# The zero margin of a DRAM table moved from GpSimd's queue to SyncE's, and the first image's normalized rows split over VectorE and ScalarE

## The chip, the core and the metric

The kernel runs on one core of a Trainium2 chip. The core has TensorE (PE), VectorE (DVE), ScalarE (ACT), GpSimd (POOL) and SyncE (SP), and 16 DMA engines that move data between DRAM and the core's SBUF. SP computes nothing: it issues DMAs. POOL issues DMAs too, through a queue of its own. The metric is the device time of the whole program in microseconds (us).

## The reference

The network takes four images of 256 channels by 64 by 64 positions and applies four residual blocks to each. Each block normalizes its input by groups of eight channels and adds a layer's output to the image. Cut to what matters here, the first block is:

```python
def _gn(v, G=32, eps=1e-5):                    # (g - mean) / sqrt(var + eps) by groups of 8 channels
    ...
def _L0_conv_ref(x, offset_w, offset_b, mod_w, mod_b, weight):   # K2 = 9 taps
    offset = _conv(x, offset_w, offset_b)      # 3x3 convolution, 18 channels: a shift per tap
    mask = 2.0 * sigmoid(_conv(x, mod_w, mod_b))
    return _deform_conv2d(x, offset, mask, weight)   # bilinear samples at shifted places, zero outside

x = x + _L0_conv_ref(_gn(x), ...)   # layer 0, deformable convolution
x = x + _L1_conv_ref(_gn(x), ...)   # layer 1, attention
x = x + _L2_conv_ref(_gn(x), ...)   # layer 2, deformable, in groups
x = x + _L3_conv_ref(_gn(x), ...)   # layer 3, a state-space scan
```

A sample of layer 0 blends the four neighbours of a fractional place. Places beyond the image count as zeros.

## The kernel before

Channels lie on the 128 partitions, in two halves `ct` (0 and 1). The image `x` stays in SBUF as 128 x 2 x 4096 floats. The images are computed one after another. For images 1 to 3 layer 0's preparation is done inside the layers of the image before (`known` is set). For image 0 nothing is known, and the preparation stands at the very start of the program. The change concerns that start.

The start of image 0 goes as follows.

1. `fetch` (L109) issues 16 DMAs of 256 KB on SP's queue, each 128 rows of 2 KB: eight chunks of `x`, two channel halves each. Behind them on the same queue come `ident`, `gmat`, `goff` and `base` (L138, L90), then the offset convolution's weights `l0`, the deformable convolution's weights `l0w` (128 x 4608 floats) and layer 1's weights `l1`.
2. `borders` (L114) zeroes the margin of `tab`, a table in DRAM of 4,547 rows of 1,024 floats. The rows hold, for each place of the zero-padded 66 x 66 image, the channels of its four neighbours. The first `FAR` = 67 rows and the 67 rows from row 4,480 are the margin. The source is a zeroed tile `zero` of 67 partitions by 256 floats, read four times for each row. POOL issues the two DMAs.
3. `note` (L218) takes statistics of each chunk of `x` on DVE as it lands. `stats` joins them with two small matmuls (L254, L269), a square root on ACT (L273) and a reciprocal on DVE (L274).
4. `scaled` (L289) writes the normalized rows into the padded image `xnp` with 16 DVE instructions, each of 8 rows and one channel half.
5. `table` (L406 to L414), called for t0 = 0, 5, ..., 30, transposes 5 x 128 places on PE, copies them to a tile `vt` (of which there are two) on ACT and DVE, and writes `vt` four times to `tab`, at row offsets that make the four neighbours. SP issues these 7 x 4 = 28 DMAs of 640 KB, in rows of 1 KB. The offset convolution (`offsets`, L371, two rounds of 72 matmuls here) stands between the transposes of t0 = 10 and 15, and of t0 = 20 and 25.
6. `biases` (L128) loads small constants of layer 2 through POOL (`pick`, `halves`, `bom3v`, `bv3v`). Their tiles take the place of the `vt` tiles, so the DMA of `halves` waits until all table writes have landed.
7. `along` (L489) gathers rows of `tab` by indirect DMAs that POOL issues, and the rest of layer 0 follows from these.

The order of the start on each engine is fixed by a scheduler when the program is built; at run time the engines wait for each other by semaphores. DMAs that SP issues use eight completion semaphores in turn: a DMA waits until the one issued eight before it on the queue has landed. A DMA that writes rows of `tab` that an earlier one wrote waits for it as well. The four writes of t0 = 0 start at rows 67, 66, 1 and 0, so the second of them overlaps the first margin and waits until that has landed.

Of the kernel before, what the change touches and what calls it, by code (L numbers as in the profile page):

```python
# [9 lines left out]
F32 = mybir.dt.float32  # L10
I32 = mybir.dt.int32
BF16 = mybir.dt.bfloat16
AF = mybir.ActivationFunctionType
ALU = mybir.AluOpType
AX = mybir.AxisListType

P = 128
H = W = 64
N = H * W
PW = 66  # L20
FAR = PW + 1
# [3 lines left out]
FT = -(-PW * PW // P)  # L25
# [38 lines left out]
class Net:  # L64
# [7 lines left out]
    def __init__(self, ctx: ExitStack, tc: tile.TileContext, ins: dict[str, bass.AP]):  # L72
        self.tc, self.nc, self.ins = tc, tc.nc, ins
        nc = tc.nc
        self.cpool = ctx.enter_context(tc.tile_pool(name="const", bufs=1))
        self.xpool = ctx.enter_context(tc.tile_pool(name="x", bufs=1))
        self.small = ctx.enter_context(tc.tile_pool(name="small", bufs=2))
        self.dram = ctx.enter_context(tc.tile_pool(name="dram", bufs=2, space=bass.MemoryType.DRAM))

        self.x = self.xpool.tile([P, 2, N], F32, tag="x", name="x")  # L80
        self.fetched = False
        self.fetch()
        self.eps = self.cpool.tile([P, 1], F32, tag="eps", name="eps")
        nc.gpsimd.memset(self.eps, 1e-5)
        self.ones = self.cpool.tile([P, P], F32, tag="ones", name="ones")
        nc.gpsimd.memset(self.ones, 1.0)
        for name in ("ident", "gmat", "goff"):
            setattr(self, name, self.load(self.cpool, name))
        self.base = self.cpool.tile([P, 8, 18], F32, tag="base", name="base")
        nc.sync.dma_start(out=self.base, in_=ins["base"][:, 0:8, :])  # L90
        self.first = self.spot(self.cpool, 0)
        self.awake = False
        self.omax = self.cpool.tile([P, 1], F32, tag="omax", name="omax")
        nc.gpsimd.memset(self.omax, 0.0)

        self.halves = self.cpool.tile([3, 3, P], BF16, tag="halvesb", name="halvesb")
        self.noted = None


        self.tab = self.dram.tile([FAR + FT * P, 1024], F32, tag="tab", name="tab", bufs=1)  # L100
        self.known = None
        self.pick = None
# [11 lines left out]
    def borders(self):  # L114

        nc = self.nc
        with self.tc.tile_pool(name="zero", bufs=1) as pool:
            zero = pool.tile([FAR, 1, 256], F32, tag="zero", name="zero")
            nc.gpsimd.memset(zero, 0.0)
            for r in (0, FT * P):  # L120
                nc.gpsimd.dma_start(
                    out=self.tab[r : r + FAR, :].rearrange("p (s c) -> p s c", s=4),
                    in_=zero.to_broadcast([FAR, 4, 256]),
                )

    def biases(self):

# [207 lines left out]
    def layer0(self, x, weights):  # L335


        nc, tc = self.nc, self.tc
        tab, known, self.known = self.tab, self.known, None
        with (  # L340
# [11 lines left out]
            if not known:  # L352
                for r in borders:
                    nc.gpsimd.memset(r, 0.0)
                self.borders()
                self.scaled(x, lambda ct: [(self.inner(ct, r, 8), r, 8) for r in range(0, H, 8)])
            cw, cb = self.loads(px, "l0", nc.gpsimd if known else None)
            wf = self.load(pa, "l0w")
            weights()
            spots = [self.first] + [self.spot(pa, i) for i in range(1, 4)]  # L360
# [72 lines left out]
            with (  # L433
# [16 lines left out]
                if known:  # L450
                    put = lambda q, do: after.setdefault(q, []).append(do)
                    gm, rs = known
# [1609 lines left out]
```

## Time and profile before

| | us |
|---|---|
| median of three runs | 8874.15 (8865.99 to 8879.99) |
| the profiled execution, its own time | 8914.06 |
| span of the profiled execution on the core | 8912.3 |
| busy: PE, DVE, POOL, ACT | 8069.4, 7767.5, 6963.3, 4998.0 |
| statistics of the last chunk of `x` begin (L218) | 24.54 and 25.56 |
| the 16 DVE instructions of `scaled` (L289) | 29.21 to 36.59 |
| first and last issue of a table write (L414) | 37.32 and 84.56 |
| `halves` is issued by POOL (L138) | 94.21 |
| first gather is issued (L489) | 96.01 |

Times in the profile run from the start of the span. A row of the timeline gives the start, the duration, the engine, the line of the code, the operation with what it writes and reads, and the count of merged instructions. SPq marks DMAs that SP issues; the duration is that of issuing, not of the transfer. The profiled execution is longer than the median of the runs by 0.45%.

### The profile page before, as it was taken

How to read it: one execution, taken by the hardware profiler on the slowest of the kernel's cores; microseconds unless marked ns; L12 is line 12 of the kernel's file. 1: busy time of each engine (PE TensorE's matmuls, PEld its weight loads, DVE VectorE, ACT ScalarE, POOL GpSimd, SP SyncE). 2: the span in 40 equal slices, each digit the busy share in tenths (PEclk: the TensorE clock that was granted, in tenths of full speed). 3: DMA queues.
4: the chain of work that ended last, by engine and by line, in shares of the span. 5: the costliest groups of instructions: out<-in, count | busy, mean ns of one | idle time of the engine just before them, and what ended most of it. 6: DMA issues, size and time to landing. Idle time of an engine off the chain costs nothing.

```text
span 8912.3 us, 97084 instructions
## 1 busy us (share of the span) xinstructions
PE 8069.4 (91%) x31127; PEld 4255.1 (48%) x31127; DVE 7767.5 (87%) x9908; ACT 4998.0 (56%) x7610; POOL 6963.3 (78%) x4415
## 2 busy tenths in 40 slices
PE   5789998998878999999887899999988799999997
PEld 4653474443555347444356435634435643564443
DVE  5778798999877879899987887999997778889998
ACT  4753435666675343666667434376666743446664
POOL 4747697999674779799967577989996747788998
PEclk8999999999999999999999999999999999999999
DMA  8850011445884011244588301124458820112332
GB/s 298 309 196 12 31 61 57 112 111 142 297 311 160 10 37 59 65 114 113 156 297 319 122 13 43 60 80 112 110 170 307 315 80 1 47 61 76 107 107 80
DMA packets 457945, 1149.69 MB, mean 129 GB/s; under 512 B 51426, under 2 KB 119019, under 8 KB 446161
## 3 DMA queue, kind: packets, MB, share of 16 engines
q0 software_dynamic: 178800, 681.04, 23.1%
q1 hardware_dynamic: 278624, 462.37, 16.8%
q8 instruction: 248, 4.06, 0.2%
q14 instruction: 273, 2.23, 0.1%
HBM read 905.84 MB, written 88.10 MB: 112 GB/s over the span
## 4 chain that ended last, share of the span: by engine, by line
DVE 32%; PE 32%; POOL 13%; issue 11%; ACT 5%; DMA 5%; SPq 2%; another core or an unknown queue 1%; DVEq 0%; POOLq 0%; ACTq 0%
DVE h L1886 16%; PE cx L715 10%; DVE h L1802 6%; POOL h L1909 5%; DMA g<-tab,idx 3%; PE sc L685 3%; PE pm L595 3%; PE pz L537 3%; POOL g L489 2%; PE pacc L1039 2%; SPq L892 2%; DVE prod L1014 2%; DVE r L500 2%; ACT r L499 1%; PE y L1763 1%
## 5 line engine op out<-in xcount | busy, mean ns | idle before, releaser
L1909 POOL TENSOR_TENSOR h<-h,cn 128x2048 f32<-128x2048 f32 x508 | 2300.2, 4528 | 41.3
L1886 DVE TENSOR_TENSOR_SCAN h<-da,carry,h 128x512 f32<-128x512 f32 x1636 | 1983.0, 1265 | 77.7 <-ACT da L1884 28.5
L1884 ACT ACTIVATE da<-delta,l3a 128x512 f32<-128x512 f32 x2048 | 1397.4, 691 | 1053.2 <-DVE h L1886 1049.4
L1763 PE MATMUL y<-h,ident 128*128 128x512 f32 x4096 | 1913.5, 600 | 5.1 <-POOL h L1909 4.0
L489 POOL DMA_INDIRECT g<-tab,idx x1152 | 1364.1, 1184 | 564.8 <-DVE r L500 288.4
L709 POOL TENSOR_TENSOR acc<-acc,e 128x1024 f32<-128x1024 f32 x472 | 1109.9, 2352 | 352.7 <-ACT e L700 333.7
L537 PE MATMUL pz<-cols,l0w 128*128 128x256 f32 x4608 | 1207.4, 406 | 154.0 <-DVE cols L526 77.7
L1763 PEld LDWEIGHTS y<-h,ident 128*128 128x128 f32 x4096 | 780.7, 192 | 1013.1 <-issue 946.5
L500 DVE SCALAR_TENSOR_TENSOR r<-g,wx,r 128x512 f32<-128x512 f32 x1152 | 859.4, 746 | 324.6 <-ACT r L499 198.5
L537 PEld LDWEIGHTS pz<-cols,l0w 128*128 128x128 f32 x4608 | 875.9, 201 | 360.2 <-issue 123.8
L700 ACT ACTIVATE e<-e 128x1024 f32<-128x1024 f32 x512 | 542.2, 1059 | 898.6 <-DVE e L699 785.7
L715 PE MATMUL cx<-e,v 128*128 128x512 f32 x2048 | 1002.1, 615 | 2.3 <-ACT e L700 2.3
L1802 DVE TENSOR_TENSOR h<-du,bn 128x1536 f32<-128x1536 f32 (+1 forms) x512 | 937.4, 1831 | 4.0 <-PE bn L1787 3.9
L499 ACT ACTIVATE r<-g,wx 128x512 f32<-128x512 f32 x1152 | 828.1, 719 | 195.9 <-DMA g<-tab,idx 153.5
L1014 DVE TENSOR_TENSOR prod<-ring,A 128x768 f32<-128x768 f32 (+1 forms) x640 | 715.6, 1160 | 49.3 <-DMA ring<-ring 29.5
L699 DVE TENSOR_TENSOR e<-sc,mr 128x512 f32<-128x512 f32 x1024 | 638.5, 681 | 126.6 <-PE sc L685 126.6
L1039 PE MATMUL pacc<-ident,prod 128*128 128x128 f32 x5120 | 663.9, 280 | 49.9 <-POOL prod L1028 19.4
L608 DVE TENSOR_REDUCE m<-pm 128x1 f32<-128x512 f32 x896 | 555.5, 682 | 110.8 <-PE pm L595 110.8
L519 PE MATMUL pt<-ident,acc 128*128 128x128 f32 x2304 | 420.5, 290 | 254.2 <-DVE acc L510 191.8
L715 PEld LDWEIGHTS cx<-e,v 128*128 128x128 f32 x2048 | 350.2, 189 | 603.5 <-issue 435.3
L1039 PEld LDWEIGHTS pacc<-ident,prod 128*128 128x128 f32 x5120 | 562.5, 142 | 139.8 <-POOL prod L1028 50.6
L509 ACT ACTIVATE acc<-r,wy 128x256 f32<-128x256 f32 x1152 | 574.5, 499 | 40.5 <-DVE r L500 38.7
(307 smaller groups left out, 11989.1 us busy)
## 6 DMA issues: line engine op xcount, KB each, us to landing
cn<-cd SPq DMA_DIRECT2D x512, 256.0 KB
bs<-cd SPq DMA_DIRECT2D x412, 256.0 KB
delta<-du POOLq DMA_DIRECT2D x48, 1024.0 KB
tab<-vtnext SPq DMA_DIRECT2D x192, 256.0 KB
ring<-ring SPq DMA_DIRECT2D x288, 126.0 KB
ring<-ring SPq DMA_DIRECT2D x288, 120.0 KB
delta<-w POOLq DMA_DIRECT2D x24, 1024.0 KB
g<-tab,idx POOLq DMA_INDIRECT x1152
```

The lines of the kernel that those rows point to most:

```text
L489: nc.gpsimd.indirect_dma_start(out=g[:], out_offset=None, in_=tab[:, :], in_offset=bass.IndirectOffsetOnAxis(ap=spots[t // 8][0][:, t % 8, ...
L499: nc.scalar.mul(r, g[:, :, 0, :], wx[:, 0, t, k : k + 1])
L500: nc.vector.scalar_tensor_tensor(r, g[:, :, 1, :], wx[:, 1, t, k : k + 1], r, ALU.mult, ALU.add)
L537: nc.tensor.matmul(sums[m][:, ot, :256], wf[:, i, bass.ts(ot, P)], cols[m][:, i, :], start=(i == 0), stop=(i == 17),)
L709: nc.gpsimd.tensor_add(b["acc"], b["acc"], e)
L715: nc.tensor.matmul(blocks[qb]["cx"], v[:, 4 * (i + kt // 4 * 4) + kt % 4, :], e[:, bass.ts(i % 2, 512)], start=(kt == 0 and i == 0), stop= ...
L1039: nc.tensor.matmul(d["pd"][:, ct, t, :], prod[:, x, t, bass.ts(ct, P)], self.ident, is_transpose=True, start=(wy == 0 and x == left[0] and ...
L1763: nc.tensor.matmul(c["ys", dc], self.ident, h[:, dc, :], start=False, stop=(n == DS - 1))
L1802: nc.vector.tensor_mul(h[:, :d, :], c["du"][:, :d, :], c.pop(("bn", n)).to_broadcast([P, d, C]))
L1884: nc.scalar.activation(da, c["delta"][:, dc, :], AF.Exp, scale=al[:, dc, n : n + 1])
L1886: nc.vector.tensor_tensor_scan(h[:, dc, :], da, hb, carry[:, dc, n : n + 1], ALU.mult, ALU.add)
L1909: nc.gpsimd.tensor_mul(h, h, cn.to_broadcast([P, 4, C]))
```

## The change

`zero` becomes a tile of the constants' pool with 64 floats on each of 67 partitions, zeroed once by POOL at the start. `borders` is called later, after the load of `l0`, and SP issues its two DMAs, each reading the 64 zeros 16 times for each row. On SP's queue they stand behind `x`, `ident`, `gmat`, `goff`, `base` and `l0`, and ahead of `l0w`, `l1` and the 28 table writes. POOL's two margin DMAs are gone, and its DMA of `pick` moves up.

The normalized rows of image 0 are shared: channel half 0 stays on DVE with 8 instructions, half 1 goes to ACT as 8 activations `scale * x + shift`, with a small DVE instruction that computes the shift `-mean * rs`. ACT and DVE copies of `vt`, and the small steps of the offsets, change places among each other on their engines by a few positions. PE's order is the same, and so is the order of every engine after the start. The code for the general layer 2, which the program only runs under a condition, changes in the same way.

```diff
@@ __init__
         self.awake = False
+        self.zero = self.cpool.tile([FAR, 1, 64], F32, tag="zero", name="zero")
+        nc.gpsimd.memset(self.zero, 0.0)
         self.omax = self.cpool.tile([P, 1], F32, tag="omax", name="omax")
@@ def borders(self):
-        with self.tc.tile_pool(name="zero", bufs=1) as pool:
-            zero = pool.tile([FAR, 1, 256], F32, tag="zero", name="zero")
-            nc.gpsimd.memset(zero, 0.0)
-            for r in (0, FT * P):
-                nc.gpsimd.dma_start(
-                    out=self.tab[r : r + FAR, :].rearrange("p (s c) -> p s c", s=4),
-                    in_=zero.to_broadcast([FAR, 4, 256]),
-                )
+        for r in (0, FT * P):
+            nc.sync.dma_start(
+                out=self.tab[r : r + FAR, :].rearrange("p (s c) -> p s c", c=64),
+                in_=self.zero.to_broadcast([FAR, 16, 64]),
+            )
@@ def layer0
             if not known:
                 for r in borders:
                     nc.gpsimd.memset(r, 0.0)
+                gm, rs = self.stats(x)
+                shift = self.small.tile([P, 2], F32, tag="known", name="known")
+                nc.vector.scalar_tensor_tensor(shift, gm, -1.0, rs, ALU.mult, ALU.mult)
+                for r in range(0, H, 8):
+                    for ct in range(2):
+                        to, m = self.inner(ct, r, 8), rs[:, ct : ct + 1]
+                        xs = x[:, ct, r * W : (r + 8) * W].rearrange("p (h w) -> p h w", w=W)
+                        if ct:
+                            nc.scalar.activation(to, xs, AF.Identity, bias=shift[:, ct : ct + 1], scale=m)
+                        else:
+                            nc.vector.tensor_scalar(to, xs, gm[:, ct : ct + 1], m, ALU.subtract, ALU.mult)
+            cw, cb = self.loads(px, "l0", nc.gpsimd if known else None)
+            if not known:
                 self.borders()
-                self.scaled(x, lambda ct: [(self.inner(ct, r, 8), r, 8) for r in range(0, H, 8)])
-            cw, cb = self.loads(px, "l0", nc.gpsimd if known else None)
             wf = self.load(pa, "l0w")
```

## The prediction

> **What bounds the kernel now.** The change touches only the start of image 0, so the question is what that start waits for. I read the chain of waits in order of time first (start, duration, what).
>
> ```profile
> span 8912.3 us, 97084 instructions
> ```
> ```profile
> 9.15 15.37 DMA x<-in_x
> ...
> 28.67 1.18 issue
> 29.85 6.28 PE pc L406 x30
> 36.14 15.63 PE po L371 x144
> ...
> 84.56 8.65 DMA tab<-vt
> 93.69 0.52 issue
> 94.21 0.53 POOL halves L138
> ```
>
> Up to 24.5 us the chain is the image's arrival, at its end it is a table write. Between them it runs over the offset matmuls, but the stretches of the profile (busy time by engine, then granted clock, DMA share, GB/s) say that the table writes set the pace there:
>
> ```profile
> 18.00:25.00 7.00, 0.00 (x0) 0.00 (x0) 2.54 (x4) 0.00 (x0) 0.00 (x0) 1.00 0.58 148
> 38.00:93.00 55.00, 34.99 (x320) 13.61 (x312) 16.21 (x67) 10.00 (x25) 0.00 (x0) 0.88 1.02 335
> ```
>
> From 38 to 93 us the 16 DMA engines are full. The 28 writes land at 40.69 to 93.21 us, one each 1.94 us on average, without a pause. So the start ends when the table DMAs end, and these can only move as a block. From 18 to 25 us the DMA engines are little used although the kernel waits for `x`. The timeline of SP's queue and of POOL shows why:
>
> ```profile
> 0.75 9.97 SPq L109 DMA_DIRECT2D x<-in_x  x16
> 12.47 0.33 SPq L138 DMA_DIRECT2D ident<-in_ident  x1
> ...
> 20.81 0.33 SPq L138 DMA_DIRECT2D l<-in_l  x1
> 22.90 0.33 SPq L138 DMA_DIRECT2D l0w<-in_l0w  x1
> 24.54 0.33 SPq L138 DMA_DIRECT2D l<-in_l  x1
> 37.32 48.99 SPq L414 DMA_DIRECT2D tab<-vt  x28
> ```
> ```profile
> 1.78 2.83 POOL L121 DMA_DIRECT2D tab<-zero  x1
> 3.99 3.64 POOL L121 DMA_DIRECT2D tab<-zero  x1
> ```
>
> The trace records a semaphore update for each of the 16 DMA engines of a transfer. For the last chunk of `x`, 14 engines had finished at 17.89 us, the 15th at 19.96 and the 16th at 25.27. The margin's packets (134 of 4 KB, some 160 ns each) form two streams, each a single file: one engine carries all of a margin, since its first margin's last update is at 24.29 us and the 15th at 16.59. Those two engines hand out margin and `x` packets in turn, and `x` waits for them.
>
> **The change part by part.**
>
> *POOL loses two margin DMAs* (2.83 and 3.64 us of issuing) and a 0.31 us memset, and gains one smaller memset. POOL then waits anyway, so its own time counts for nothing:
>
> ```profile
> POOL halves L138 <- DMA tab<-vt: 86.0, 1, 86.0
> ```
>
> The gain is that `x` lands when the 14 undisturbed engines had it, 17.9 us: 7.4 us earlier for everything that follows it. `pick` moving up costs nothing under the same wait.
>
> *The normalized rows are shared.* Before, 16 DVE instructions took 7.38 us (29.21 to 36.59). Now DVE has 8, 3.7 us. ACT gets 8 of 128x512; its nearest row with a scale by partition is the 0.72 us of L499, so 5.8 us, plus 0.2 us for the new shift (the 128x2 DVE rows take 0.16). ACT's `vt` copies stand behind its 8 activations, so the first table is complete about 6.0 + 1.5 = 7.5 us after the start of normalizing, against 8.1 before: a gain of 0.6 us at most, and what it feeds is late below. I count 0. The cover is the margin on SP's queue, and without it the load of `l0w`; without either up to 0.6 us would be gained.
>
> *The margin goes through SP.* It now stands ahead of `l0w`, `l1` and all 28 table writes, on the same rings of the same engines; the second table write also waits for the first margin's landing, SP issues in order, and behind the last table write wait POOL's `halves` and all gathers. So every us in which the margin holds an engine is a us for all of these. Two numbers decide.
>
> First, over how many engines it spreads. The source has 67 partitions, the destination 1072 pieces. On SP's queue, the ring copies of layer 2 (1065 to 1085 us) show in their updates 15 engines for 60 rows, 9 for 63, 2 for 2: the largest divisor up to 16. 67 is prime, so one engine, as the margin did on POOL's queue. The nearest count in the trace, 63 rows on 9 engines, would give 39.0/9 - 10.5 = -6 us by the sum below. The Trainium skill, DMA: Bandwidth & Descriptors, "Why a DMA increments its semaphore by 16 and not by 1", speaks against the change: it takes the largest count up to 16 that divides the slowest dimension of both sides, which is 1 here and +28 us; no row of this trace shows 67 rows on SP's queue.
>
> Second, the price c of a piece. A piece is now 256 B (it was 1 KB, carried in 4 KB packets). No such piece is in the trace. The records on SP's queue are 9 ns for 4 B, 27 ns at least for 512 B, 46 ns for 1 KB (the table writes), 84 ns for 2 KB: 9 ns and 0.036 ns for each byte, so 18.2 ns for 256 B. The bounds are 9 ns (a 4 B record) and 46 ns (the nearest record that is written to DRAM); I take 18.2, on the line between 4 B and 512 B.
>
> The Trainium skill weighs this otherwise. DMA: Bandwidth & Descriptors, "Why small descriptors are slow", gives a 256 B piece 27% over line rate, and its table 27 GiB/s an engine, which I estimate at 12.1 ns and a sum of +15 us instead of +28. Its "Specifications" say that pieces under 512 B cost a read-modify-write, with no price, which speaks against this change.
>
> Now the sum, in the profiled execution's time. `x` is in at 17.9; the constants ahead of the margin (560 KB at about 335 GB/s) take 1.7: 19.6. The margins take 2 x 1072 x 18.2 ns = 39.0 us on one engine: 58.6. SP meanwhile can't run ahead: in the table stage it holds about three DMAs (some 115 pieces an engine) in flight and then blocks, so it is stuck in the margin until about 56 us, and `l0w` and `l1` come after it on all engines. They took 7.4 + 1.1 us before (the 14 engines' updates at 23.46, 30.87 and 31.97): 67.1. Then the table block, whose data began at about 38.6 before (first landing 40.69 less one write and its receipt). It starts 28.5 us later and has the same length. The compute is ready far earlier: `x` at 17.9 gives the first table at about 29, and the offset rounds, 15.6 us each, fit below the writes. So the sum is 19.6 + 2144 c + 8.5 - 38.6 = 2144 c - 10.5 us, +28.5 for 18.2 ns. (If SP didn't block, the one engine alone, with 8 packets of 686 ns of `l0w` and 8 of 141 ns of `l1`, gives +26.6.) Everything after the first gather keeps its order and moves as a block, since the program is one sequence.
>
> The profiled span would go from 8912.3 to 8940.8. Runs without the profile have a median of 8874.15, 0.45% below the profiled 8914.06; the start's share of that is under 1 us, so the same 28.5 us are added: 8902.6.
>
> **The rivals.** A difference under 0.2% (17.7 us) can hardly be told from no change.
>
> 1. *The margin spreads, and the change is not slower.* Were the destination's 1072 rows to set the count, 16 engines would share 2144 pieces: 2.4 us. The sum is then 39.0/k - 10.5 us: -8.1 for k = 16, and zero or less from k = 4. For it: 1072 is 67 times 16. Against it: 63 rows got 9 engines, so the partition count of a source binds, and the old margin, 67 against 268, used one engine. Time 8866.
>
> 2. *One engine, but cheap pieces.* At 9 ns the sum is +8.8 us (8883); up to 13.2 ns it stays within 0.2%. Against it: 512 B pieces show no less than 27 ns.
>
> 3. *One engine, dear pieces.* Written to DRAM, a 256 B piece may cost as much as one of 1 KB: 46 ns, 98.6 us, +88 (8962). At 27 ns, as for 512 B, it is +47 (8922), at twice my price +68 (8942).
>
> **How the numbers follow.** One engine at 13.2 to 36.4 ns is the forecast, 0.68; dearer 0.08; cheaper 0.08; spread over several engines 0.13; anything that shortens the table block itself, which alone could gain over 0.2%, 0.03. So slower 0.76, same 0.21, faster 0.03. The range takes in rival 1 (8866, with 2 us for the runs' scatter 8864) and the forecast up to twice the price (8942): 0.89 of the chance. Rival 3 beyond that is left out.
>
> **What would show it.** Right: the last statistics begin near 17.9 us; SP's two margin issues take about 17 and 19 us; between 25 and 55 us the DMA share falls to about 1/16 with some 14 GB/s; the 28 table writes keep 1.94 us each but land until about 122; the first gather moves from 96.0 to about 124.5, and later distances are unchanged. Wrong: margin issues under 1 us and table writes from about 30 us (rival 1); an idle stretch of under 25 us or over 75 us (rivals 2 and 3); a shift that grows or shrinks after the first gather.

## The result, and the profile after

Over 20 runs of each kernel the changed kernel has a median of 8887.98 us (8875.63 to 8909.09) and the kernel before 8876.44 us (8862.69 to 8890.58). The ratio is 1.0014, with a 95% interval of 1.0009 to 1.002: 12.4 us slower by the ratio, between 8 and 18 (the medians lie 11.5 us apart). That is inside the 0.2% that the prediction called no change, in the direction that it forecast, and less than half of the 28.5 us.

The profiled execution of the changed kernel took 8879.76 us, less than the 8914.06 of the one before. This is no gain of the change. The stage from the first to the last gather of an image lasted 478.6, 482.4, 480.1 and 482.5 us for the four images of the execution before, and 467.2, 470.2, 465.2 and 469.2 after, for code that is the same. From the last gather of one image to the first of the next it is 1715 to 1724 us in both. Single executions scatter by the gathers, so the change is read from the start alone, and its time from many runs.

This is SP's queue in the timeline after (start, duration of issuing, line, transfer, count):

```profile
0.74 9.45 SPq L111 DMA_DIRECT2D x<-in_x  x16
10.55 0.33 SPq L137 DMA_DIRECT2D ident<-in_ident  x1
...
13.20 0.33 SPq L137 DMA_DIRECT2D l<-in_l  x1
13.95 15.46 SPq L120 DMA_DIRECT2D tab<-zero  x2
29.45 15.04 SPq L137 DMA_DIRECT2D l0w<-in_l0w  x1
44.54 0.42 SPq L137 DMA_DIRECT2D l<-in_l  x1
45.08 54.15 SPq L424 DMA_DIRECT2D tab<-vt  x28
```

The constants go out 1.9 to 7.6 us sooner, because `x` is in sooner. Then SP stands still: the two margin DMAs and the `l0w` behind them take until 44.5 us to issue, and the first table write goes out at 45.08 instead of 37.32. The stretches of the same execution (busy time by engine, granted clock, DMA share, GB/s) show what moves meanwhile:

```profile
10.00:15.00 5.00, 0.00 (x0) 0.00 (x0) 5.00 (x8) 0.00 (x0) 0.00 (x0) 1.00 1.06 369
16.00:45.00 29.00, 24.08 (x196) 12.21 (x196) 6.50 (x18) 8.19 (x14) 0.00 (x0) 1.00 0.08 19
53.00:106.00 53.00, 21.99 (x174) 8.28 (x174) 16.27 (x67) 9.35 (x24) 0.00 (x0) 0.69 1.04 350
```

Until 15 us all DMA engines carry `x` and, at the end, constants. From 16 to 45 us the 16 engines are used to 0.08, a little over one engine in 16: the margin. Its semaphores count two updates for each of the two DMAs, one at issue and one at the landing, so each has one engine. Its 2144 pieces of 256 B follow each other without a pause from 15.84 to 46.11 us. The compute is long done when SP is free: in the next rows (DVE and ACT, the shared normalized rows) all rows are written by 25.23 us.

```profile
19.30 3.74 DVE L364 TENSOR_SCALAR xnp<-x,gm,rs 128x512 f32<-128x512 f32 x8
```
```profile
19.47 5.76 ACT L362 ACTIVATE xnp<-x,known,rs 128x512 f32<-128x512 f32 x8 [0.48 <-DVE known L356]
25.13 1.58 ACT L419 COPY vt<-pc 128x512 f32<-128x512 f32 x4
```

POOL's rows show the end of the start. The wait for the table writes is 103.8 us, and the first gather comes at 108.91 us instead of 96.01:

```profile
107.04 0.54 POOL L137 DMA_DIRECT2D halves<-in_halves  x1 [103.80 <-DMA tab<-vt]
...
108.91 1.05 POOL L499 DMA_INDIRECT g<-tab,idx  x1 [0.30 <-issue]
```

The first gather is 12.9 us later and the runs are 12.4 us longer.

### The profile page after: what moved, and what is told of

It reads as the page before. It is cut to its first block, busy times and chain, and to the rows that moved or that the text cites. A ratio compares the mean times of both kernels' runs of the same rounds, so it can differ in the third digit from the quotient of the medians.

```text
span 8878.0 us, 97080 instructions
## 1 busy us (share of the span) xinstructions
PE 8072.3 (91%) x31127; PEld 4264.0 (48%) x31127; DVE 7765.3 (87%) x9901; ACT 4992.2 (56%) x7618; POOL 6929.9 (78%) x4413
## 3 DMA queue, kind: packets, MB, share of 16 engines
q1 hardware_dynamic: 280770, 462.92, 16.7%
## 4 chain that ended last, share of the span: by engine, by line
DVE 34%; PE 31%; POOL 12%; issue 9%; ACT 5%; DMA 4%; SPq 3%; another core or an unknown queue 1%; DVEq 0%; POOLq 0%; ACTq 0%
DVE h L1896 17%; PE cx L725 11%; DVE h L1812 7%; POOL h L1919 6%; PE sc L695 3%; PE pz L547 3%; PE pm L605 3%; DMA g<-tab,idx 3%; DVE r L510 2%; DVE acc L520 2%; SPq L902 2%; PE pacc L1049 2%; DVE prod L1024 1%; ACT r L509 1%; POOL prod L1038 1%
## 5 line engine op out<-in xcount | busy, mean ns | idle before, releaser
L499 POOL DMA_INDIRECT g<-tab,idx x1152 | 1331.0, 1155 | 546.2 <-DVE r L510 266.1
```

The costliest lines, as they stand in the source:

```text
L499: nc.gpsimd.indirect_dma_start(out=g[:], out_offset=None, in_=tab[:, :], in_offset=bass.IndirectOffsetOnAxis(ap=spots[t // 8][0][:, t % 8, ...
```

## The experiments

The measure of the start is the time of the first gather (96.01 us before, 108.91 after). Ratios are to the kernel before on the same chip. Twelve runs follow; four of them repeat an earlier kernel, and its first gather came within about 0.3 us of the earlier one. Where no ratio is given, the kernel was executed once, and only its start is read.

**The two parts apart.** First the sharing of rows alone, on the kernel before:

```diff
-                self.scaled(x, lambda ct: [(self.inner(ct, r, 8), r, 8) for r in range(0, H, 8)])
+                gm, rs = self.stats(x)      # and the DVE/ACT loop of the change; borders() stays as before
```

> The kernel before with only the normalized rows shared between VectorE and ScalarE; the margin stays on GpSimd's queue. Theory (one DMA engine is held by the margin, the sharing is hidden): the last statistics stay near 24.5 us, the first table write is issued at about 36.7 us instead of 37.32, and the first gather at 95.4 to 96.0 us (96.01 before); time within 0.1% of before. Rival (the sharing has a part in the 12.9 us that the first gather moved): the first gather moves by 2 us or more in either direction.

Measured: first table write issued at 36.40 us, first gather at 95.05, ratio 0.9993 (0.9983 to 1.0003). The start gained 1.0 us, a little more than the theory's 0.6 and less than the rival's 2. The first table write goes out 6.7 us after the start of normalizing, where the prediction had 7.5 and the kernel before 8.1; normalizing itself began 0.5 us later than before. No time can be read from so little.

Then the margin alone:

```diff
-                gm, rs = self.stats(x)      # and the DVE/ACT loop
+                self.scaled(x, lambda ct: [(self.inner(ct, r, 8), r, 8) for r in range(0, H, 8)])
```

> The changed kernel with all normalized rows back on VectorE; the margin stays on SyncE's queue. Theory: the first gather at 108.9 us within 0.5 us, as in the changed kernel (108.91), ratio to before about 1.0014, since the table is ready at about 28 us and the margin holds the queue until 46. Rival (sharing matters): the first gather below 107 or above 111 us.

Measured: first gather at 108.97 us, as forecast; ratio 1.0000 (0.999 to 1.0011), which leaves out the 1.0014 that was expected. So the sharing has no part in the 12.9 us, but the time was not as late as the gather. The last group of runs returns to this.

**Is it the single engine?** The same bytes at the same place of SP's queue, cut so that 16 engines can share them:

```diff
-        self.zero = self.cpool.tile([FAR, 1, 64], F32, tag="zero", name="zero")
+        self.zero = self.cpool.tile([P, 1, 134], F32, tag="zero", name="zero")
...
-                out=self.tab[r : r + FAR, :].rearrange("p (s c) -> p s c", c=64),
-                in_=self.zero.to_broadcast([FAR, 16, 64]),
+                out=self.tab[r : r + FAR, :].rearrange("p c -> (p c)").rearrange("(q s c) -> q s c", q=P, c=134),
+                in_=self.zero.to_broadcast([P, 4, 134]),
```

> The changed kernel with the same margin bytes cut over 128 partitions of 4 pieces of 536 B, so that all 16 DMA engines can share them, at the same place on SyncE's queue. Theory (it is the single engine that costs): 64 pieces an engine at 27 ns, under 2 us; image in at 15.3, margin done near 17.6, weights by 26, first table write issued near 27, first gather between 83 and 86 us, 10 to 13 us before the kernel before; ratio about 0.9987. Rival (it is the place on SyncE's queue, whatever the spread): the first gather stays at 96 us or later.

Measured: first gather at 84.90 us, ratio 0.9984 (0.9974 to 0.9994). SP's queue and POOL's first gather in its timeline:

```profile
13.96 1.33 SPq L120 DMA_DIRECT2D tab<-zero  x2
15.34 0.66 SPq L137 DMA_DIRECT2D l0w<-in_l0w  x1
16.04 0.82 SPq L137 DMA_DIRECT2D l<-in_l  x1
26.02 49.17 SPq L424 DMA_DIRECT2D tab<-vt  x28
```
```profile
84.90 1.21 POOL L499 DMA_INDIRECT g<-tab,idx  x1 [0.30 <-issue]
```

Once the margin is spread, its place on SP's queue holds no table write up: the first goes out at 26.02 us, as soon as the first table is ready (ACT's second copy ends at 25.99). The margin's pieces take from 15.46 to 20.18 us, longer than the forecast 2 us, and the last weights land beside the first table write, at 28.07; a microsecond or two could still lie there. Its ratio is below 1 and below the 1.0014 of the change.

The same spread on POOL's queue, in the kernel before, tests why `x` was late there:

```diff
-            zero = pool.tile([FAR, 1, 256], F32, tag="zero", name="zero")
+            zero = pool.tile([P, FAR * 1024 // P], F32, tag="zero", name="zero")
...
-                    out=self.tab[r : r + FAR, :].rearrange("p (s c) -> p s c", s=4),
-                    in_=zero.to_broadcast([FAR, 4, 256]),
+                    out=self.tab[r : r + FAR, :].rearrange("p c -> (p c)").rearrange("(q f) -> q f", q=P),
+                    in_=zero,
```

> The kernel before with the same margin bytes cut over 128 partitions of 2144 B, still on GpSimd's queue at the start, normalization on VectorE alone. Theory (the image was late because two engines were shared with the margin): the image is in at 16 to 17.5 us instead of 25.3, and the first gather at 85 to 88 us. Rival (writes to DRAM beside the image's loads, or GpSimd's queue itself, hold the image up): the image stays later than 20 us.

Measured: the last packet of `x` ends at 16.58 us (24.85 before) and the first gather comes at 87.78. So neither writes beside the loads nor POOL's queue as such held `x` up, but the form of this margin did: in it two engines carry all of the data. The other engines were slowed as well, by small packets that came with it (see the account of the prediction). Its issuing is short too, compared with 2.83 and 3.64 us before:

```profile
2.01 0.73 POOL L121 DMA_DIRECT2D tab<-zero  x1
2.74 0.43 POOL L354 MEMSET xnp<- 128x380 f32 x1
3.09 0.56 POOL L121 DMA_DIRECT2D tab<-zero  x1
```

The ratio is 0.9995 (0.9984 to 1.0005): the 8.2 us of the start (0.0009) lie inside, and so does no change.

**The count of engines.** One more row at each end makes 68 rows, which four divides:

```diff
-        for r in (0, FT * P):
+        for r in (0, FT * P - 1):
...
-                out=self.tab[r : r + FAR, :].rearrange("p (s c) -> p s c", c=64),
-                in_=self.zero.to_broadcast([FAR, 16, 64]),
+                out=self.tab[r : r + FAR + 1, :].rearrange("p (s c) -> p s c", c=64),
+                in_=self.zero.to_broadcast([FAR + 1, 16, 64]),
```

> The changed kernel with a margin of 68 rows instead of 67 at each end (the extra row is written again by table writes); pieces of 256 B as before, 1.5% more bytes. Theory (the count of engines is the largest divisor up to 16 that both sides' rows share): four engines with 544 pieces each, 7.7 us instead of 30.3; first gather at 85 to 88 us. Rival (the engine is one for another reason, such as the source being read repeatedly): the first gather stays near 109 us.

Measured: five semaphore updates for each margin DMA, one at issue and four landings. The pieces run from 16.02 to 24.25 us, 8.2 us instead of 30.3, and the first gather comes at 87.90. Its rows:

```profile
14.27 4.88 SPq L120 DMA_DIRECT2D tab<-zero  x2
19.19 3.85 SPq L137 DMA_DIRECT2D l0w<-in_l0w  x1
```
```profile
87.90 1.05 POOL L499 DMA_INDIRECT g<-tab,idx  x1 [0.30 <-issue]
```

With 1.5% more bytes the start is 21 us shorter than with 67 rows. The divisor decides, not the repeated source.

**The price of a piece.** Pieces of 512 B (`zero` of 128 floats, read 8 times) and of 128 B (32 floats, read 32 times), on one engine:

```diff
-                out=self.tab[r : r + FAR, :].rearrange("p (s c) -> p s c", c=64),
-                in_=self.zero.to_broadcast([FAR, 16, 64]),
+                out=self.tab[r : r + FAR, :].rearrange("p (s c) -> p s c", c=128),
+                in_=self.zero.to_broadcast([FAR, 8, 128]),
```

> The changed kernel with the margin's pieces of 512 B instead of 256 B: half as many pieces, the same bytes, still 67 partitions and so one engine. Theory with a price by piece and byte, read as the spacing of pieces (256 B: 14.1 ns; the 512 B records last 27 ns): 1072 pieces at 20 to 27 ns, 21 to 29 us on the engine instead of 30.3, first gather between 100 and 108 us (108.91 with 256 B). Rival, a fixed price of 14 ns a piece: 15 us and a first gather near 94 us. Rival, a price by bytes alone: no change from 108.9.

> The changed kernel with pieces of 128 B: twice as many pieces, the same bytes, one engine. Theory (what the engine is held for is passed on one to one): the first gather moves by as much as the margin's stretch on the engine grows. With a price of 9.5 to 14 ns a piece, 4288 pieces hold it 41 to 60 us instead of 30.3, and the first gather comes at 119 to 139 us. Rival (the bytes decide, or the delay is hidden in part behind the compute): the first gather stays within 3 us of 108.9, or moves by less than half of what the stretch grows.

| piece | pieces | record lasts | pieces follow each other after | on the engine | first gather |
|---|---|---|---|---|---|
| 512 B | 1072 | 27 ns | 23.5 ns | 25.2 us | 103.62 us |
| 256 B (the change) | 2144 | 18 ns | 14.1 ns | 30.3 us | 108.91 us |
| 128 B | 4288 | 14 ns | 11.7 ns | 50.1 us | 129.41 us |

The time on the engine comes from the first to the last packet. From 256 to 128 B it grows by 19.9 us and the first gather moves by 20.5; from 256 to 512 B it shrinks by 5.1 and the gather comes 5.3 sooner. What the engine is held for is passed on one to one. Neither a fixed price for a piece nor a price by bytes alone fits the three rows.

**Is the delay passed on to the end?** Four kernels on one chip: the change, the 128 B pieces, the margin alone, and the spread margin, each as above.

> The changed kernel itself, on the same chip as the next three. Theory (the delay of the first gather is passed on to the end): the first gather near 108.9 us, 12.9 us late, ratio to before 1.0014 (plus 12 to 13 us). Rival (the gather stage of image 0 gives most of a delay back, as one execution of it lasted 467 us instead of 479): the first gather as late, but the ratio 1.000 to 1.0005, and the gather stage of image 0 shorter than before by about 11 us.

> The changed kernel with margin pieces of 128 B, timed. Theory: first gather near 129.4 us, 33.4 us late, ratio about 1.0038 (plus 33 us). Rival (given back in the gather stage): ratio below 1.0026, with a gather stage of image 0 of about 464 us.

> The changed kernel with all normalized rows on VectorE, once more beside the changed kernel. Theory: ratio 1.0014 as the changed kernel, within the intervals of both. Rival (the sharing of the rows costs time somewhere behind the start): the changed kernel is slower than this one by more than 0.1%.

> The changed kernel with the margin cut over 128 partitions, beside the changed kernel. Theory: first gather near 84.9 us, 11 us early, ratio about 0.9988, and about 24 us below the changed kernel. Rival (given back in the gather stage): ratio 0.9995 to 1.0, less than 10 us below the changed kernel.

| kernel | first gather, us | against 96.01 | ratio, 95% interval |
|---|---|---|---|
| the change | 108.66 | +12.7 | 1.0006, 0.9996 to 1.0015 |
| 128 B pieces | 129.10 | +33.1 | 1.0036, 1.0023 to 1.0049 |
| margin alone | 109.05 | +13.0 | 1.0010, 1.0001 to 1.0019 |
| spread margin | 85.13 | -10.9 | 0.9988, 0.9978 to 0.9998 |

SP's queue with 128 B pieces shows the longest standstill, by its two rows:

```profile
14.08 25.23 SPq L120 DMA_DIRECT2D tab<-zero  x2
39.36 25.13 SPq L137 DMA_DIRECT2D l0w<-in_l0w  x1
```

The largest shift, 33.1 us (0.0037), appears whole in the time, 1.0036 (20 to 44 us by the interval), and the spread's -10.9 us (-0.0012) as 0.9988. The median of the spread version is 23.9 us under that of the change (8868.51 against 8892.41), where the first gathers differ by 23.5; by the two ratios it is 16 us. The margin's own shift of about 12.9 us has been timed four times, twice in each form: 1.0014, 1.0006, 1.0010 and 1.0000. Their mean is 1.0008, 7 us. Three intervals hold 1.0014, that of the first run of the margin alone does not. No cost of the sharing behind the start is seen: the ratio of the change is 0.0004 below that of the margin alone, its median 4.0 us (0.0005) above; a difference below 0.1% can't be told here. Whether some of the 12.9 us is given back is open, but the gather stage of image 0 does not show it. On this chip it lasted 465, 464 and 458 us after the three late starts and 464 after the early one (the spread margin). In the other executions it lasted 464 to 475 us where the first gather came after 100 us, and 455 to 479 where it came before: no order by lateness.

**Does the sharing pay once the margin is spread?** The spread version with all rows on DVE:

```diff
-                gm, rs = self.stats(x)      # and the DVE/ACT loop
+                self.scaled(x, lambda ct: [(self.inner(ct, r, 8), r, 8) for r in range(0, H, 8)])
```

> The changed kernel with the margin cut over 128 partitions on SyncE's queue and all normalized rows on VectorE: the spread version without the sharing. Theory (once the margin no longer holds the queue, the table writes wait for the first finished table, and the sharing shows): first table write issued about 8.1 us after the start of normalizing, near 27.4 us instead of 26.0, first gather 1 to 2 us later than the 84.9 us of the spread version with sharing. Rival (the loads of weights still hide it): first gather within 0.4 us of 84.9.

Measured: normalizing starts at 19.88 us, the first table write is issued at 27.93, the first gather at 86.48, 1.6 us later than with the sharing.

```profile
27.93 48.84 SPq L414 DMA_DIRECT2D tab<-vt  x28
```

The first write goes out 8.05 us after the start of normalizing, with the sharing 6.69 us (19.33 to 26.02). So the sharing is worth 1.4 us there; some 0.5 us of the 1.6 between the first gathers come from `x`, which landed that much later here. It shows only when the margin no longer covers it.

## Why the prediction was right or wrong

*The bound.* Right: the table writes form one block that ends the start; it kept its length between 52.7 and 55.1 us in all runs (54.6 before) while its beginning moved between 27 and 73 us.

*`x` is held up by the margin's two engines.* Right for the last chunk, which 14 engines had at 17.89 us and the last one at 25.27. The gain was mis-sized: without this margin `x` is in at 15.25 us, not at 17.9, so the 14 engines had been disturbed too. Beside the margin's 134 packets of 4 KB POOL's queue carried 2010 packets of 16 B from 7.99 us on, 15 for each packet of 4 KB. From 9 to 16 us a 2 KB packet of `x` lasted 116 ns (median), against 84 in the change and in the version spread on POOL's queue, which have no such packets. A 256 KB chunk then landed every 1.0 us, against 0.67. The stretch from 9 to 14 us, before and after, and POOL's queue in it before (packets, MB, share of the 16 engines):

```profile
9.00:14.00 5.00, 0.00 (x0) 0.00 (x0) 2.23 (x4) 0.00 (x0) 0.00 (x0) 1.00 1.15 276
9.00:14.00 5.00, 0.00 (x0) 0.00 (x0) 5.00 (x9) 0.00 (x0) 0.00 (x0) 1.00 1.05 389
```
```profile
q0 software_dynamic: 736, 0.10, 19.2%
```

SP did not hold these engines back: it issued the last chunk at 10.39 us, only 0.5 us later than in the change. What the 16 B packets are for, the runs don't show.

*One engine.* Right, by the updates of the change and by 68 rows on four engines. Rival 1 (spread over 16) falls for the change; its time came true in the version that was cut to spread, 10.9 and 11.1 us early against its 8.1.

*The price.* This is the term that was most mis-sized: 18.2 ns were taken, 14.1 were measured, 30.3 us on the engine instead of 39.0. The record of a 256 B packet does last 18 ns, as interpolated from the records' durations. But the next one starts after 14, so small packets overlap, and a duration is not the spacing. The estimate from the Trainium skill, DMA: Bandwidth & Descriptors, "Why small descriptors are slow", 12.1 ns, was nearer to the spacing, and the measurement stands between the two. (The page's 27% are 3 of 11 cycles: the estimate is 11/8 of the line rate's time, not 1.27 times.) A read-modify-write below 512 B, as its "Specifications" has it, can't be told apart here: 256 B go through at 18 GB/s and 512 B at 22, and no run shows a price for it by itself. Rival 2 (cheap pieces within 0.2%) asked for at most 13.2 ns and so came close; rival 3 (dear ones) falls.

*The sum.* Each term, predicted and measured, in us:

| term | predicted | measured | difference |
|---|---|---|---|
| margin's first piece | 19.6 | 15.8 | -3.8 |
| margin on its engine | 39.0 | 30.3 | -8.7 |
| from there to the table's first packet | 8.5 | 7.0 | -1.5 |
| table block's start before, subtracted | 38.6 | 38.2 | +0.4 |
| length of the block, against 54.6 before | same | 52.7 | -1.9 |

Together with 0.1 us less from the block's end to the first gather, these take 28.5 to 12.9. All the errors but one point the same way. The first comes from `x`; of the third about 1.0 us is that `l0w` starts at 45.11 us, while the margin's last pieces still run. The sum holds in form, with another constant: the time on the engine less the delay of the first gather is 17.6, 17.4 and 16.7 us for 512, 256 and 128 B, where the prediction had 10.5.

*The chances.* The forecast put 0.76 on slower by over 0.2% and 0.21 on less; the time came out in the second class, 8887.98 us, inside the range of 8864 to 8942. It did not get there by one of the two ways that the 0.21 stood for (pieces of at most 13.2 ns, or a spread): at 14.1 ns the prediction's own sum still gives 19.7 us, over 0.2%. The earlier `x` and the smaller terms made up the rest. The time lies below the forecast's own lower end (13.2 ns, +17.8 us); the range holds it because it was stretched down for a spread margin, and that part is luck.

*What would show it.* The first margin DMA took 0.85 us to issue and the second 14.55, and `l0w` 15.04; 17 and 19 were forecast for the margins. SP handed over the first margin whole and was blocked with the next transfer until all but 110 to 118 pieces of the one ahead had started (95 to 99 with 128 B pieces). The total standstill is as reasoned, but it shows one row lower, at the DMA behind.

*The shared rows.* Right for the change: hidden, as the margin alone has the same first gather. Where the margin does not hide them they are worth 1.4 us, not 0.6 at most, from the start of normalizing to the first write (8.1 to 6.7 us, with the margin on POOL's queue as with the spread one). The first write waits for two of ACT's copies, 0.8 us (25.16 to 25.99 in the spread version), where 1.5 were taken. The load of `l0w`, which was named as the second cover, hid nothing.

## What to carry to other kernels

Before moving a DMA to another queue, ask how many engines its shape lets it use, and look at the semaphore updates: a leading dimension that no number from 2 to 16 divides (67 rows) puts all of it on one engine, and everything behind it on an in-order queue waits for that engine. Cutting the same bytes over 128 partitions made 11 us of gain at the start out of a 13 us loss. Where the start of a long program moves, read its last event in the profile, because single executions of this kernel scatter by more than the effect.

## What the runs showed of the hardware that was not expected

- Small packets on one DMA engine overlap: 14.1 ns from one 256 B packet to the next with records of 18 ns, 23.5 against 27 for 512 B, 11.7 against 14 for 128 B.
- A copy from 67 partitions on POOL's queue kept two engines busy with its data and slowed the rest as well: 2010 packets of 16 B came with its 134 of 4 KB, and a 2 KB packet of the image lasted 116 ns beside them, 84 without. Cut over 128 partitions, the same bytes went as 128 packets of 4,288 B and none of 16 B.
- In the change the first seven table writes landed 1.70 us apart, the later ones 1.9 on average (1.6 to 3.1), and every kernel whose margin went through SP on one engine or four had a block of 52.7 to 53.5 us instead of 54.5 to 55.1. The stretch from 53 to 66 us shows the rate:

```profile
53.00:66.00 13.00, 3.99 (x18) 1.73 (x22) 4.47 (x19) 3.19 (x7) 0.00 (x0) 0.50 1.08 383
66.00:100.00 34.00, 18.00 (x160) 6.55 (x152) 11.80 (x48) 6.15 (x17) 0.00 (x0) 0.80 1.04 344
```

383 GB/s, then 344. From 53 to 65 us every 1 KB packet of the table lasts 46 ns; later, and through the whole block of the kernel before, the median is 48 and one or two in a hundred last 80 ns or more. The cause stays open; nothing was tried for it.
